# A hybrid block with a state space layer: the skip term, one normalization and the gate's buffers move

## The chip, the cores and the metric

The kernel runs on one core of a Trainium2 chip. A core has TensorE (PE: matrix products, with PEld for its loads of the stationary operand), VectorE (DVE), ScalarE (ACT), GpSimd (POOL) and SyncE (SP, which here issues most DMAs). PSUM is the memory that TensorE writes, used here as eight banks of 128 x 512 f32: two each under the tags A, B, C and T. The metric is the device time of one execution in microseconds. Runs are summed up by their median; one further execution was recorded by the profiler.

## The reference

Input x has 2 sequences of 2048 tokens with 256 features. Four residual layers follow each other, each on a normalized x: a state space layer, a mixture of 8 experts of which each token takes 2, an attention over a pair of tokens (over the two sequences), and the same mixture of experts again. Only the first layer is changed:

```python
zxbcdt = einsum('bld,ed->ble', layernorm(x), W_in)      # z: 512, xBC: 768, dt: 8
xBC = silu(causal_depthwise_conv(xBC, conv_w, conv_b))  # four taps
x, B, C = xBC[:512] as 8 heads of 64, xBC[512:640], xBC[640:]
dt = softplus(dt + dt_bias)
h_t = h_{t-1} * exp(dt * A) + (dt * x_t) B_t            # per head, state of 64 x 128
y = h_t C_t
y = y + D * x                                           # the skip: one number D per head
y = y * silu(z)                                         # the gate
y = y * rsqrt(mean(y * y) + eps) * norm_w
out = y @ W_out.T
```

## The kernel before

All of it is f32. Tokens are worked on in groups of 512 (TG), of four chunks of 128. There are eight groups, in the order (sequence 0, part 0), (sequence 1, part 0), (sequence 0, part 1) and so on (`order`), so 32 chunks, here counted from 0.

`project` makes a group ready. It normalizes x (`layernorm`: statistics and `xn` on VectorE, the power for `rs` on GpSimd), transposes `xn` on TensorE (`pt`, copied to `xT` by ScalarE), computes `dt` with a polynomial on VectorE, and then for six blocks of 128 channels the projection (`pc`, L1000), two copies of it on ScalarE (L1007, L1009), three taps of the convolution on VectorE (L1018) and a silu on ScalarE (L1026). The result is `xc`, with channels on the partitions.

`chunk_front` prepares one chunk: the gate `sz` = silu(`pz`) on ScalarE (L1050), the decay matrices `lt` of the eight heads (L1055, L1058, L1089), and `px`, the transpose of x to tokens on the partitions. VectorE reads `px` twice: `dtx` = dt * x (L1067) and `xd` = D * x (L1069). GpSimd makes `wx` from `dtx` (L1082).

`chunk_back` computes the chunk's output. `py` is C times the state (L1098), scaled into `y` by VectorE (L1100). The state `h` is scaled by GpSimd (L1109) and the product `ph` added by VectorE (L1111). `pi` is the product of `lt` and `dtx`, one matmul per head (L1114). Then GpSimd adds `xd` to `y` (L1121), VectorE adds `pi` (L1123), and GpSimd multiplies with `sz` (L1124). `chunk_out` squares `y` on ScalarE (L1133), transposes it (`pty`) and multiplies it with `W_out` (`po`), and VectorE adds the result to x (L1151).

The main loop interleaves by hand: per chunk it emits steps of the next group's `project` (`aside`), the front of the next chunk, the back of this one, and the output of the one before. Once a group is through the layer, `routing` chooses the experts of its tokens, and eight scatters per group (L438, GpSimd's queue) enter them in a table. These scatters are emitted by `late.step()`, one or none at each GpSimd step of a chunk. From about the fifth group on, expert tiles that are already full are computed between the chunks (`tiles.step()`; up products `pab` L727, down products `pf` L757, gate `gT` L736), 21 of them early.

SP's instructions stay in the program's order. Those of the other engines are put in order by a scheduler when the kernel is built; every engine then works through its own list in that order. Tiles come from pools with a number of buffers for each tag: `s2` has two unless `bufs` says otherwise. A tile's buffer comes free when all readers of its former content are done, so the number of buffers decides who waits.

Of the kernel before, what the change touches and what calls it, by code (L numbers as in the profile page):

```python
# [17 lines left out]
GT = 4  # L18
# [4 lines left out]
DI = 512  # L23
NH, HD = 8, 64
# [22 lines left out]
def kernel(  # L47
# [24 lines left out]
    nc = tc.nc  # L72
# [7 lines left out]
    lnp = ctx.enter_context(tc.tile_pool(name="ln", bufs=2))  # L80
# [6 lines left out]
    order = [(b, s) for s in range(NS) for b in range(NB)]  # L87
    xg, xr = {}, {}
# [22 lines left out]
    ident = const.tile([P, P], F32, name="ident")  # L111
# [47 lines left out]
    dsk = load_const("dsk", [P, NH], d_skip.partition_broadcast(P))  # L159
# [70 lines left out]
    def pool(i):  # L230
        on_pool[:] = [i.ins]


    normed, turned = [], []


    def layernorm(x, name):

        st = lnp.tile([P, GT, 6], F32, tag="st", name=f"st_{name}")
        mv = lnp.tile([P, GT, 2], F32, tag="mv", name=f"mv_{name}")  # L240
        for t in range(GT):
            nc.vector.bn_stats(st[:, t, :], x[:, t, :])
            nc.vector.bn_aggr(mv[:, t, :], st[:, t, :])
        yield
        rs = lnp.tile([P, GT], F32, tag="rs", name=f"rs_{name}")
        nc.vector.tensor_scalar(rs, mv[:, :, 1], EPS, None, ALU.add)  # L246
        pool(nc.gpsimd.tensor_tensor(rs, rs, mhalf, ALU.pow))  # L247
        yield
        xn = lnp.tile([P, GT, DM], F32, tag="xn", name=f"xn_{name}")
        for t in range(GT):  # L250
            i = nc.vector.tensor_scalar(
                xn[:, t, :], x[:, t, :], mv[:, t, 0:1], rs[:, t : t + 1], ALU.subtract, ALU.mult
            )
            normed[:] = [i.ins]
        return xn, rs, mv[:, :, 1]
# [606 lines left out]
    with tc.tile_pool(name="ssm1", bufs=1) as s1, tc.tile_pool(name="ssm2", bufs=2) as s2:  # L862
# [20 lines left out]
        def route_out():  # L883
# [23 lines left out]
                w_out_sb[:, :, DM:], pw[:, : DI // P * NE].rearrange("p (c n) -> p c n", n=NE)  # L907
            )

        sums = {g: tc.dram_tile([GT * NH, P], F32, name=f"sums{g[0]}{g[1]}") for g in order}  # L910
        tails, state = {}, {}
        for b in range(NB):
# [4 lines left out]

        def project(b, s):
            nm = f"{b}{s}"
            xn, rs, var = yield from layernorm(xg[b, s], f"a{nm}")  # L920
            yield
            xT = s2.tile([P, KD, TG], F32, tag="xT", name=f"xT_{nm}")
            transpose_group(xT, xn, f"a{nm}")
# [5 lines left out]
            for t in range(GT):  # L929
                for k in range(KD):  # L930
# [4 lines left out]
                        start=(k == 0),  # L935
                        stop=(k == KD - 1),
# [19 lines left out]
            r = s2.tile([P, GT, NH], F32, tag="r", name=f"r_{nm}")  # L956
# [5 lines left out]
            g = s2.tile([P, GT, NH], F32, tag="g", name=f"g_{nm}")  # L962
# [32 lines left out]
            xc = s2.tile([P, NC, TG], F32, tag="xc", name=f"xc_{nm}")  # L995
            nc.gpsimd.tensor_copy(pre[:, :, 0 : KC - 1], tails[b])
            for c in range(NC):
                pc = bank("A", f"pc_{nm}_{c}")
                for k in range(KD):
# [4 lines left out]
                        start=(k == 0),  # L1004
# [35 lines left out]
        def chunk_front(b, s, t, g, lb):  # L1040
            nm = f"{b}{s}{t}"
            xc, ts = g["xc"], slice(t * P, (t + 1) * P)
            per_head = [P, NH, HD]


            pz = bank("A", f"pz_{nm}")
            for k in range(KD):
                nc.tensor.matmul(pz, g["xT"][:, k, ts], w_in_sb[:, k, 0:DI], start=(k == 0), stop=(k == KD - 1))
            sz = s2.tile([P, DI], F32, tag="sz", name=f"sz_{nm}")
            nc.scalar.activation(sz, pz, AF.Silu)  # L1050


            lt = s2.tile([P, NH, P], F32, tag="lt", name=f"lt_{nm}", bufs=3)
            for i in range(NH):
                nc.scalar.activation(  # L1055
                    lt[:, i, :], lb[:, i, :], AF.Relu, bias=g["cum"][:, t, i : i + 1], scale=-1.0
                )
            nc.scalar.activation(lt, lt, AF.Exp, scale=-1.0)  # L1058


            px = bank("T", f"px_{nm}")
            for c in range(DI // P):
                nc.tensor.transpose(px[:, c * P : (c + 1) * P], xc[:, c, ts], ident)
            pxh = px.rearrange("p (h d) -> p h d", h=NH)
            dtx = s2.tile([P, DI], F32, tag="dtx", name=f"dtx_{nm}")
            dtxh = dtx.rearrange("p (h d) -> p h d", h=NH)
            nc.vector.tensor_tensor(dtxh, pxh, g["dt"][:, t, :].unsqueeze(2).to_broadcast(per_head), ALU.mult)  # L1067
            xd = s2.tile([P, DI], F32, tag="xd", name=f"xd_{nm}")
            nc.vector.tensor_tensor(  # L1069
                xd.rearrange("p (h d) -> p h d", h=NH), pxh, dsk.unsqueeze(2).to_broadcast(per_head), ALU.mult  # L1070
            )
            pb = bank("B", f"pb_{nm}")
            nc.tensor.transpose(pb[:, 0:P], xc[:, 4, ts], ident)
            nc.tensor.matmul(pb[:, P : 2 * P], xc[:, 4, ts], xc[:, 5, ts], start=True, stop=True)
            bt = s2.tile([P, P], F32, tag="bt", name=f"bt_{nm}")
            nc.scalar.copy(bt, pb[:, 0:P])
            gm = s2.tile([P, P], F32, tag="gm", name=f"gm_{nm}")
            nc.vector.tensor_tensor(gm, pb[:, P : 2 * P], tri, ALU.mult)


            wx = s2.tile([P, DI], F32, tag="wx", name=f"wx_{nm}")
            pool(nc.gpsimd.tensor_tensor(  # L1082
                wx.rearrange("p (h d) -> p h d", h=NH),
                dtxh,
                g["dec"][:, 2, t, :].unsqueeze(2).to_broadcast(per_head),
                ALU.mult,
            ))
            late.step()
            nc.vector.tensor_tensor(lt, lt, gm.unsqueeze(1).to_broadcast([P, NH, P]), ALU.mult)  # L1089
            return dict(lt=lt, dtx=dtx, xd=xd, bt=bt, wx=wx, sz=sz)  # L1090

        def chunk_back(b, s, t, g, f):
            nm = f"{b}{s}{t}"
            ts = slice(t * P, (t + 1) * P)
            per_head = [P, NH, HD]
            h = state[b]
            py = bank("C", f"py_{nm}")
            nc.tensor.matmul(py, g["xc"][:, 5, ts], h, start=True, stop=True)  # L1098
            y = s2.tile([P, DI], F32, tag="y", name=f"y_{nm}", bufs=3)
            nc.vector.tensor_tensor(  # L1100
                y.rearrange("p (h d) -> p h d", h=NH),
                py.rearrange("p (h d) -> p h d", h=NH),
                g["dec"][:, 0, t, :].unsqueeze(2).to_broadcast(per_head),
                ALU.mult,
            )
            ph = bank("C", f"ph_{nm}")
            nc.tensor.matmul(ph, f["bt"], f["wx"], start=True, stop=True)
            hh = h.rearrange("p (h d) -> p h d", h=NH)
            pool(nc.gpsimd.tensor_tensor(hh, hh, g["dec"][:, 1, t, :].unsqueeze(2).to_broadcast(per_head), ALU.mult))  # L1109
            late.step()  # L1110
            nc.vector.tensor_tensor(h, h, ph, ALU.add)  # L1111
            pi = bank("C", f"pi_{nm}")
            for i in range(NH):
                nc.tensor.matmul(  # L1114
                    pi[:, i * HD : (i + 1) * HD],
                    f["lt"][:, i, :],
                    f["dtx"][:, i * HD : (i + 1) * HD],
                    start=True,
                    stop=True,
                )  # L1120
            pool(nc.gpsimd.tensor_tensor(y, y, f["xd"], ALU.add))  # L1121
            late.step()
            nc.vector.tensor_tensor(y, y, pi, ALU.add)  # L1123
            pool(nc.gpsimd.tensor_tensor(y, y, f["sz"], ALU.mult))  # L1124
            late.step()
            return y

        def chunk_out(b, s, t, y):
            nm = f"{b}{s}{t}"

            yt = s2.tile([P, DI], F32, tag="yt", name=f"yt_{nm}")
            ss = s2.tile([P, 1], F32, tag="ss", name=f"ss_{nm}")
            nc.scalar.activation(yt, y, AF.Square, accum_out=ss)  # L1133
            nc.vector.tensor_scalar(ss, ss, 1.0 / DI, EPS, ALU.mult, ALU.add)
            pool(nc.gpsimd.tensor_tensor(ss, ss, mhalf[:, 0:1], ALU.pow))
            late.step()
# [3 lines left out]
            nc.scalar.copy(yt, pt)  # L1140
            po = bank("T", f"po_{nm}")
            for c in range(DI // P):
                nc.tensor.matmul(
                    po[:, 0 : DM + NE],
                    yt[:, c * P : (c + 1) * P],
                    w_out_sb[:, c, :],
                    start=(c == 0),
                    stop=(c == DI // P - 1),
                )
            x = xr[b, s][:, t, :]  # L1150
            nc.vector.scalar_tensor_tensor(x, po[:, 0 : DM + NE], ss, x, ALU.mult, ALU.add)  # L1151

# [402 lines left out]
```

## Time and profile before

| | us |
|---|---|
| median of 3 runs | 1716.64 (1710.98 to 1721.71) |
| the profiled execution's own time | 1689.27 |
| its span, first to last instruction | 1687.6 |
| PE busy over the span | 1579.0 |
| DVE busy | 896.0 |
| ACT busy | 672.3 |
| POOL busy | 740.2 |
| DMA queues: moved | 231.30 MB |

The profile's page gives busy times by engine, then the span in 40 slices of 42 us with the busy share in tenths, and then groups of like instructions. A line of such a group has the line of the program, the engine, the operation, what it writes and reads, how often, its busy time in us and the mean ns of one, and then the idle time of the engine just before it with what ended that. A matmul of f32 operands shows as two records, each with its load. The first layer ends at about 700 us, with the early expert tiles in its second half; the first expert layer ends before 900 us, the attention runs to about 1400 us beside the second layer's early tiles, and the second expert layer fills the rest.

### The profile page before, as it was taken

What the parts mean: (1) busy time and instruction counts of PE and PEld (TensorE: products, weight loads), DVE (VectorE), ACT (ScalarE), POOL (GpSimd) and SP (SyncE); (2) the same over time, 40 slices, a digit from 0 to 9 for tenths busy, and PEclk for the clock granted to TensorE, in tenths of its full rate; (3) what the DMA queues carried; (4) which work ended last, traced back from release to release, by engine and by line L of the source; (5) the groups of instructions that cost most, each with busy time, mean ns of one, the idle gap of its engine ahead of it and who ended that gap; (6) DMA issues with size and microseconds to landing.
All of it is one profiled execution on the core that took longest, in us unless ns stands there. A gap on an engine that the chain in (4) does not pass through costs nothing.

```text
span 1687.6 us, 22145 instructions
## 1 busy us (share of the span) xinstructions
PE 1579.0 (94%) x7088; PEld 1189.4 (70%) x7088; DVE 896.0 (53%) x2471; ACT 672.3 (40%) x1338; POOL 740.2 (44%) x702
## 2 busy tenths in 40 slices
PE   6997987999999999999998999899999999999997
PEld 4665555676677777788984566475767878888886
DVE  6777978847648364422227658548454622222222
ACT  5786867856647543232322202002020322323332
POOL 4356457455455566644442002423150663544443
PEclk9898988999999999999999999999999999999999
DMA  4022212743535455889852321715435588878883
GB/s 170 28 59 53 89 28 61 216 126 90 141 66 177 105 144 132 214 248 327 228 123 82 67 60 52 100 51 102 144 71 142 148 222 238 227 225 231 227 220 47
DMA packets 174744, 231.30 MB, mean 137 GB/s; under 512 B 45920, under 2 KB 138080, under 8 KB 174368
## 3 DMA queue, kind: packets, MB, share of 16 engines
q1 hardware_dynamic: 143520, 193.42, 38.8%
q0 software_dynamic: 31104, 36.42, 12.3%
q8 instruction: 58, 0.95, 0.2%
q14 instruction: 62, 0.51, 0.1%
HBM read 192.72 MB, written 37.06 MB: 136 GB/s over the span
## 4 chain that ended last, share of the span: by engine, by line
PE 46%; DMA 7%; DVE 2%; POOL 1%; issue 1%; ACT 0%; SPq 0%; DVEq 0%; POOLq 0%
PE pab_g L727 9%; PE pao L1446 7%; PE pq L1352 5%; PE pab_f L727 5%; PE pf_g L757 4%; PE pab_ge L727 3%; PE pvd L1426 3%; PE pk L1352 3%; DMA out_dram<-y_g,tab_g 2%; PE pf_f L757 2%; DMA o<-prob 2%; PE pf_ge L757 1%; PE pr_g L335 1%; DMA xs_f<-xnd_f,tab_f 1%; DMA resid<-y_f,tab_f 1%
## 5 line engine op out<-in xcount | busy, mean ns | idle before, releaser
L727 PE MATMUL pab_g<-xT_g,w_g 128*128 128x256 f32 (+1 forms) x896 | 181.4, 361 | 0.0
L727 PE MATMUL pab_fe<-xT_fe,w_fe 128*128 128x256 f32 x672 | 159.0, 392 | 20.0 <-DVE gT_fe L736 16.8
L727 PEld LDWEIGHTS pab_g<-xT_g,w_g 128*128 128x128 f32 x896 | 158.4, 190 | 19.6 <-ACT xT_g L718 0.4
L727 PEld LDWEIGHTS pab_fe<-xT_fe,w_fe 128*128 128x128 f32 x672 | 129.1, 195 | 47.3 <-DVE gT_fe L736 21.5
L781 POOL DMA_INDIRECT out_dram<-y_g,tab_g x51 | 80.3, 1575 | 137.2 <-DVE y_g L770 46.3
L735 ACT ACTIVATE sa_g<-pab_g,b_g 128x256 f32<-128x256 f32 (+1 forms) x112 | 51.0, 455 | 188.0 <-PE pab_g L727 188.0
L736 DVE SCALAR_TENSOR_TENSOR gT_g<-pab_g,b_g,sa_g 128x256 f32<-128x256 f32 (+1 forms) x112 | 51.5, 460 | 129.0 <-ACT sa_g L735 127.3
L1352 PE MATMUL pq<-w_qkv_sb,axT 128*128 128x512 f32 x256 | 117.4, 597 | 0.0
L1018 DVE SCALAR_TENSOR_TENSOR xc<-pre,conv_w_sb,xc 128x512 f32<-128x512 f32 x144 | 111.5, 791 | 4.2 <-ACT xc L1009 3.5
L1446 PE MATMUL pao<-w_o_sb,o 128*128 128x256 f32 x512 | 112.3, 380 | 0.0
L1446 PEld LDWEIGHTS pao<-w_o_sb,o 128*128 128x128 f32 x512 | 97.0, 190 | 15.9 <-issue 2.6
L727 PE MATMUL pab_f<-xT_f,w_f 128*128 128x256 f32 (+1 forms) x512 | 96.4, 346 | 0.0
L1000 PE MATMUL pc<-xT,w_in_sb 128*128 128x512 f32 x192 | 94.7, 622 | 0.2 <-ACT xc L1009 0.2
L438 POOL DMA_INDIRECT table_g<-pay_g,at_g x64 | 62.3, 974 | 72.5 <-DVE w_g L414 39.5
L757 PE MATMUL pf_g<-w_g,gT_g 128*128 128x256 f32 x408 | 92.8, 379 | 0.0
L727 PEld LDWEIGHTS pab_f<-xT_f,w_f 128*128 128x128 f32 x512 | 85.4, 191 | 9.4
L1055 ACT ACTIVATE lt<-lb,cum 128x128 f32<-128x128 f32 x256 | 82.9, 393 | 18.7 <-DMA lb<-sums 18.6
L1352 PEld LDWEIGHTS pq<-w_qkv_sb,axT 128*128 128x128 f32 x256 | 48.5, 192 | 57.9 <-issue 56.0
L781 POOL DMA_INDIRECT resid<-y_fe,tab_fe x42 | 67.0, 1596 | 37.0 <-DVE y_fe L770 21.8
L1367 ACT ACTIVATE kd<-pk 128x512 f32<-128x512 f32 x32 | 19.1, 597 | 159.5 <-PE pk L1352 90.5
L757 PEld LDWEIGHTS pf_g<-w_g,gT_g 128*128 128x128 f32 x408 | 75.4, 190 | 9.3 <-DVE gT_g L736 0.2
L247 POOL TENSOR_TENSOR rs_g<-rs_g,mhalf 128x4 f32<-128x4 f32 x8 | 8.2, 1019 | 167.6 <-DVE rs_g L246 151.9
(477 smaller groups left out, 3401.2 us busy)
## 6 DMA issues: line engine op xcount, KB each, us to landing
w_g<-in_wl_dram SPq DMA_DIRECT2D x28, 1024.0 KB, 6.0
w_fe<-in_wl_dram SPq DMA_DIRECT2D x21, 1024.0 KB, 5.0
lb<-sums SPq DMA_DIRECT2D x32, 512.0 KB, 5.3
w_f<-in_wl_dram SPq DMA_DIRECT2D x16, 1024.0 KB, 5.8
o<-prob SPq DMA_DIRECT2D x32, 512.0 KB, 17.9
w_g<-in_wl_dram SPq DMA_DIRECT2D x28, 512.0 KB, 4.9
w_fe<-in_wl_dram SPq DMA_DIRECT2D x21, 512.0 KB
w_ge<-in_wl_dram SPq DMA_DIRECT2D x9, 1024.0 KB
```

The lines of the kernel that those rows point to most:

```text
L438: i = nc.gpsimd.indirect_dma_start(out=self.table, out_offset=bass.IndirectOffsetOnAxis(ap=at[:, t, c : c + 1], axis=0), in_=pay[:, t, c, ...
L727: nc.tensor.matmul(p[:, q * n : (q + 1) * n], t["w1"][:, k, c * P : (c + 1) * P], t["xT"][:, k, :], start=(k == 0), stop=(k == KD - 1),)
L735: nc.scalar.activation(sa[:, :n], p[:, 0:n], AF.Silu, bias=t["b1"][:, i : i + 1])
L736: nc.vector.scalar_tensor_tensor(t["gT"][:, i, :n], p[:, n : 2 * n], t["b1"][:, NHT + i : NHT + i + 1], sa[:, :n], ALU.add, ALU.mult)
L757: nc.tensor.matmul(pos[h][:, h * DM : (h + 1) * DM], t["gT"][:, j, h * P : (h + 1) * P], t["w2"][:, j, :], start=(j == 0), stop=(j == NHT ...
L781: j = nc.gpsimd.indirect_dma_start(out=self.acc if self.direct else self.acc[: self.seq[i][4] or NT + TT, :], out_offset=bass.IndirectOffs ...
L1000: nc.tensor.matmul(pc, w_in_sb[:, k, DI + c * P : DI + (c + 1) * P], xT[:, k, :], start=(k == 0), stop=(k == KD - 1),)
L1018: nc.vector.scalar_tensor_tensor(xc[:, c, :], pre[:, c, j : j + TG], conv_w_sb[:, c, j : j + 1], xc[:, c, :], ALU.mult, ALU.add,)
L1055: nc.scalar.activation(lt[:, i, :], lb[:, i, :], AF.Relu, bias=g["cum"][:, t, i : i + 1], scale=-1.0)
L1352: nc.tensor.matmul(p, src[:, k, t * P : (t + 1) * P], w_qkv_sb[:, k, j, half * TG : (half + 1) * TG], start=(k == 0), stop=(k == KD - 1),)
L1426: nc.tensor.matmul(pvd, w_qkv_sb[:, k, 2, c * P : (c + 1) * P], xd[:, k, :], start=(k == 0), stop=(k == KD - 1),)
L1446: nc.tensor.matmul(po[:, j * DM : (j + 1) * DM], o[i][:, c, (t + j) * P : (t + j + 1) * P], w_o_sb[:, c, :], start=(c == 0), stop=(c == NA ...
```

## The change

It has three parts.

First, for the first five groups of `order` (`SKIPS = 5`, so chunks 0 to 19) the skip is computed on TensorE. Once at the start VectorE fills `skip`, four diagonal matrices of 128 x 128 with D on the diagonal (eight instructions on 64 partitions each). In `chunk_back` a matmul of `xc` with such a matrix is put ahead of each pair of `pi`'s heads; it writes the 128 columns that the two heads then add to. For these chunks `xd` and GpSimd's addition of it are gone, and with them one `late.step()` per chunk. For the last three groups they stay, but `xd` has one buffer instead of two.

Second, the normalization in `project` computes `xn` on ScalarE as x * rs + off, with `off` = -mean * rs from one small VectorE instruction. The other normalizations stay on VectorE.

Third, `sz` has three buffers instead of two.

```diff
+        if act:
+            off = lnp.tile([P, GT], F32, tag="off", name=f"off_{name}")
+            i = nc.vector.scalar_tensor_tensor(off, mv[:, :, 0], -1.0, rs, ALU.mult, ALU.mult)
+            normed[:] = [i.ins]
         for t in range(GT):
+            if act:
+                nc.scalar.activation(
+                    xn[:, t, :], x[:, t, :], AF.Identity, bias=off[:, t : t + 1], scale=rs[:, t : t + 1]
+                )
+                continue
             i = nc.vector.tensor_scalar(
                 xn[:, t, :], x[:, t, :], mv[:, t, 0:1], rs[:, t : t + 1], ALU.subtract, ALU.mult
             )
...
+        skip = s1.tile([P, DI // P, P], F32, name="skip")
+        for i in range(NH):
+            r = slice(i % 2 * HD, (i % 2 + 1) * HD)
+            nc.vector.tensor_scalar(skip[r, i // 2, :], ident[r, :], dsk[r, i : i + 1], None, ALU.mult)
...
-            xn, rs, var = yield from layernorm(xg[b, s], f"a{nm}")
+            xn, rs, var = yield from layernorm(xg[b, s], f"a{nm}", act=True)
...
-            sz = s2.tile([P, DI], F32, tag="sz", name=f"sz_{nm}")
+            sz = s2.tile([P, DI], F32, tag="sz", name=f"sz_{nm}", bufs=3)
...
-            xd = s2.tile([P, DI], F32, tag="xd", name=f"xd_{nm}")
-            nc.vector.tensor_tensor(
-                xd.rearrange("p (h d) -> p h d", h=NH), pxh, dsk.unsqueeze(2).to_broadcast(per_head), ALU.mult
-            )
+            xd = None
+            if order.index((b, s)) >= SKIPS:
+                xd = s2.tile([P, DI], F32, tag="xd", name=f"xd_{nm}", bufs=1)
+                nc.vector.tensor_tensor(
+                    xd.rearrange("p (h d) -> p h d", h=NH), pxh, dsk.unsqueeze(2).to_broadcast(per_head), ALU.mult
+                )
...
             for i in range(NH):
+                c = i // 2
+                if f["xd"] is None and i % 2 == 0:
+                    nc.tensor.matmul(
+                        pi[:, c * P : (c + 1) * P], g["xc"][:, c, ts], skip[:, c, :], start=(i == 0), stop=False
+                    )
                 nc.tensor.matmul(
                     pi[:, i * HD : (i + 1) * HD],
                     f["lt"][:, i, :],
                     f["dtx"][:, i * HD : (i + 1) * HD],
-                    start=True,
-                    stop=True,
-                )
-            pool(nc.gpsimd.tensor_tensor(y, y, f["xd"], ALU.add))
-            late.step()
+                    start=f["xd"] is not None,
+                    stop=f["xd"] is not None or i == NH - 1,
+                )
+            if f["xd"] is not None:
+                pool(nc.gpsimd.tensor_tensor(y, y, f["xd"], ALU.add))
+                late.step()
             nc.vector.tensor_tensor(y, y, pi, ALU.add)
...
+        SKIPS = 5
```

More of the change, by code (lines that the diff above doesn't have):

```diff
@@ L234, with layernorm @@
     normed, turned = [], []
-    def layernorm(x, name):
+    def layernorm(x, name, act=False):
         st = lnp.tile([P, GT, 6], F32, tag="st", name=f"st_{name}")
```

## The prediction

> **What bounds the kernel now.** I read the page's slices first, then the table by stretches, then the waits and groups of the stage that changes. Between 0 and about 700 us lies the state space stage; everything after it is untouched.
>
> ```profile
> PE   6997987999999999999998999899999999999997
> DVE  6777978847648364422227658548454622222222
> PEclk9898988999999999999999999999999999999999
> ```
>
> A slice is 42 us. In the first seven, VectorE is as full as TensorE and the granted clock dips; from the eighth TensorE alone is at nine tenths. The chain that ended last is no help: followed back it stops at 705.8 us and has no piece before that. So I cut at the end of the addition y<-y,pi (L1123) of chunks 5, 9, 13, 17 (117.2, 181.8, 243.1, 306.7 us) and of chunks 19, 23, 27, 31. The columns are busy us (and instructions) of PE, PEld, DVE, ACT, POOL, then the clock, the DMA share and GB/s.
>
> ```profile
> 117.20:181.80 64.60, 53.73 (x236) 35.68 (x234) 53.34 (x134) 46.45 (x94) 34.24 (x32) 0.92 0.24 58
> 181.80:243.10 61.30, 53.34 (x237) 34.04 (x236) 49.09 (x130) 45.76 (x90) 33.33 (x32) 0.92 0.19 61
> 243.10:306.70 63.60, 53.29 (x234) 34.44 (x232) 55.60 (x155) 47.91 (x93) 38.99 (x36) 0.92 0.30 88
> 364.00:466.30 102.30, 94.98 (x443) 71.44 (x442) 64.16 (x168) 62.20 (x121) 53.98 (x48) 0.98 0.43 120
> 466.30:567.40 101.10, 94.60 (x444) 71.61 (x443) 61.70 (x163) 62.05 (x121) 52.97 (x46) 0.98 0.45 121
> ```
>
> A group of four chunks takes 63.2 us early: PE 53.5 busy, DVE 52.7, ACT 46.7, POOL 35.5. None is full; the pace passes between them. Late, with one early expert tile in each chunk, a group takes 101 us and PE is busy 93%: there TensorE is the bound. Where the pace goes early, the groups and waits of 60 to 300 us show:
>
> ```profile
> L438 POOL DMA_INDIRECT table_f<-pay_f,at_f x24 | 28.8, 1201 | 4.2 <-issue 4.1 <-DVE st_f L242 0.2
> L1121 POOL TENSOR_TENSOR y<-y,xd 128x512 f32<-128x512 f32 x16 | 22.3, 1395 | 5.6 <-DVE y L1100 4.9 <-ACT yt L1140 0.4
> L1123 DVE TENSOR_TENSOR y<-y,pi 128x512 f32<-128x512 f32 x16 | 10.8, 676 | 11.8 <-POOL y L1121 7.2 <-PE pi L1114 4.6
> L1069 DVE TENSOR_TENSOR xd<-px,dsk 128x512 f32<-128x512 f32 x16 | 10.9, 679 | 0.0
> L251 DVE TENSOR_SCALAR xn_a<-x,mv_a,rs_a 128x256 f32<-128x256 f32 x12 | 9.4, 827 | 0.0
> L1114 PEld LDWEIGHTS pi<-dtx,lt 128*128 128x128 f32 x256 | 33.8, 208 | 7.9 <-DVE y L1100 4.9 <-issue 2.5 <-DVE h L1111 0.2
> L1050 ACT ACTIVATE sz<-pz 128x512 f32<-128x512 f32 x16 | 9.5, 593 | 18.7 <-POOL y L1124 18.6
> ```
>
> VectorE runs without a gap through the convolution and routing of a group. Then eight routing scatters (L438) come onto POOL between the y and h steps, and POOL sets the pace: the timeline has it working almost without a gap over 142.4 to 158.4, 205.3 to 224 and 263.9 to 271.9 us, 43 of 189.5 us. In these stretches stand four additions y<-y,xd (149.2, 205.3, 216.2, 270.7), and VectorE's y<-y,pi waits for two of them, 7.2 us.
>
> **The change, per early group.**
>
> VectorE loses four xd, 4 x 0.679 = 2.7 us. It loses four xn_a: 9.4 us for 12, so 3.1 us. It gains one small off (128x4; its likeness L941 takes 0.15 to 0.39), 0.2. Sum -5.6 of 52.7. Here a rule bears: the Trainium skill, "SBUF — State Buffer", section "SBUF: two separate sides", says that a VectorE instruction using two ports and a GpSimd instruction lock each other out for a whole instruction. The trace agrees in size: xn_a has a median of 408 ns over the stage but a longest of 2470, and a mean of 827 in this stretch. By the undisturbed median the move returns 1.6 us a group, by the row with its lock-outs 3.1; I take 3.1, because the disturbed time is what the group pays. Worth something is only what lies outside the POOL-paced stretches, 146.5 of 189.5 us: 5.6 x 0.77 = 4.3.
>
> POOL loses four y<-y,xd, 4 x 1.395 = 5.6 of 35.5. On the path were four in three groups, 4 x 1.27 / 3 = 1.7. y<-y,pi then waits for PE pi alone (already last of the two for 4.6 us). POOL also steps the routing scatters one time fewer per chunk (four instead of five). In the built order they stand almost as before, 16 of them instead of 15 or 18 around chunk 15, and the first early plan falls after 15 state additions instead of 16: nothing for it. SP's queue keeps its order.
>
> ScalarE gains four 128x256 instructions with a scale and a bias per partition. Bounds: by_fe (L769, 128x256, one such operand) 0.510, xc (L1009, 128x512, two) 0.784; I take 0.55, near the first, so 2.2 us. Against this speaks the Trainium skill, "ScalarE: Activation LUTs", section "Rules for kernel authors": additions and multiplications belong on VectorE, not ScalarE. By VectorE's 0.408 the move would lose 0.6 us a group if ScalarE set the pace; by the rows ScalarE idles 16.5 of 63.2 us, and its 2.2 lie in that. They wait for rs, which POOL makes, and for off; queued behind them on ScalarE are the Square of an earlier chunk, the next lt rows and the two xT copies, for which PE waits. The like wait of xn_f on POOL was 4.8 us in three times. If the idle time were used up, this costs 2.2 + 1.6 = 3.8 a group. The third sz buffer takes away the 18.6 us that ScalarE waited in five times; ScalarE was not the last there, so it only pays for the above: nothing by itself (0 to -1).
>
> TensorE gains four f32 matmuls of 128x128x128 per chunk, that is eight records. Bounds: pi's loads in a row cost 33.8 / 256 = 0.132 each, 1.06 a chunk; the 128-column pb matmuls (L1074) 6.3 / 32 = 0.197 each, 1.6 a chunk. They stand among pi's, so I take 1.06: 4.2 a group.
>
> Now the sum. VectorE and POOL would let a group shrink by 4.3 + 1.7 = 6.0, to 57.2. TensorE would then be asked for 53.5 + 4.2 = 57.7, more than there is. The best stretch of 60 us in the stage (60 to 120) had PE busy 57.1, 95%, at clock 1.00. So TensorE is late next: at the granted 0.92 its floor is 57.7 / 0.95 = 60.7 (-2.5); at a full clock 57.7 x 0.92 / 0.95 = 55.9 (-7.3). Fewer pauses should raise the clock: from 300 to 420 us, where the first tiles fill PE's pauses, it is 1.00. I take the midpoint, -4.9. The period of four groups (54 to 307 us) gives -19.6.
>
> Start: eight small VectorE instructions for skip (0.15 to 0.44 each, by L885 and L127), about 2 us, in a spot where VectorE waited 2.2 us for x: nothing, or +2. First norm on ScalarE: +0.5, within the error.
>
> Late: chunks 18 and 19 have the four matmuls where PE is full: 2 x 1.06 = +2.1. In groups 5 to 7 xd has one buffer. xd of chunk i+1 now waits for POOL's y<-y,xd of chunk i, which waits for y<-py on VectorE itself. In the built order xd therefore stands behind that y in six of twelve chunks; queued behind it are the h addition, y<-y,pi and gT of the expert tile, for which PE waits. The wait is what POOL needs after py (h 1.15, y<-y,xd 1.27) less VectorE's own 0.68 and 0.48: 1.3 us, and once or twice an indirect DMA of 1.2 more: 10 us of VectorE idle in all. VectorE is 60 to 63% busy there and mostly waits for PE's pi anyway; bounds 0 and +10, taken +2.5. px keeps its PSUM bank longer, but the next user of that bank, po of chunk i-1, comes some 12 us later.
>
> Sum: -19.6 + 2.1 + 2.5 = -15.0 on the profiled execution (1689.3, span 1687.6). The median of the runs is 1.6% above it, 1716.6, so -15.2 there: about 1701.5.
>
> **Rivals.** (a) The clock recovers fully and VectorE with POOL sets the pace: -6.0 x 4 + 2.1 = -22, 1694. For it: the 1.00 of 300 to 420 us; against: 0.92 in all three early groups. (b) TensorE takes the place of what is removed and the clock stays: -2.5 x 4 + 2.1 + 4 = -4, 1713. This is the change not doing what it says: work moved from two engines onto a third that was as full. For it: 53.5 against 52.7 busy. (c) Slower: the single xd buffer. Price: for each of twelve chunks POOL's h, one indirect DMA and y<-y,xd, 1.15 + 1.2 + 1.4 = 3.7, or 45, standing before gT, with PE stopped as it was for 14.2 us before pab_fe for want of gT (360 to 660 us). With the early gain that is -19.6 + 2.1 + 45 = +27, 1744. It decides once a wait outlasts the matmuls that PE has queued ahead of gT (some 3.5 us of pab). Against it: six of the twelve have no wait by the order.
>
> **How the numbers follow.** 38% for the forecast (own range 1692 to 1710), 22% for (a), 20% for (b), 20% for (c), spread over 1722 to 1755. Within 1% (17 us) is about what a measurement tells from no change: the runs of before lie 11 us apart. Faster: most of (a) and four tenths of the forecast, 0.35. Slower: most of (c), 0.17. Same: 0.48. For 8 in 10 the range goes from 1687 (half of (a)'s error below it) to 1738 (half of (c) above).
>
> **What would show it.** In the early groups: a period near 58 us; xd, y<-y,xd and the wait of y<-y,pi on POOL gone; sz without its wait; PE at 95% with a clock above 0.92; the xn rows on ACT near 0.55. Late: a group still at 101 us, VectorE's wait of xd on POOL of about 10 us in all, pab_fe's wait for gT no longer than 14 us. The prediction is wrong if the early period stays at 61 or more, or a late group passes 103.

## The result, and the profile after

| | before | after |
|---|---|---|
| median of 22 runs each | 1717.37 us (1705.72 to 1723.31) | 1721.90 us (1713.76 to 1731.11) |
| ratio to before, 95% interval | | 1.0033 (1.0018 to 1.0048) |
| profiled execution, its span | 1689.27, 1687.6 | 1713.76, 1712.1 |
| VectorE busy over the span | 896.0 | 867.4 |
| POOL busy | 740.2 | 709.2 |
| PE busy | 1579.0 | 1599.3 |

The change takes 29 us off VectorE and 31 us off POOL, and the kernel is 0.3% slower. The medians lie 4.5 us apart; by the ratio the loss is 5.7 us, where a gain of 15.2 was forecast. A warning belongs beside the table: the profiled execution of before, on which the prediction was built, lies 28 us below the median of its own kernel, under the fastest of the 22 runs, so the difference of the two profiles (24.5 us) overstates the loss. A second profile of before, taken later, spans 1703.6 us; it is used below where stages are compared.

The slices of after, a slice being 43 us, show where to look:

```profile
PE   7999998999899888899998999899999899999997
DVE  6777787457466364422226757447454622222222
PEclk9999999999999899999999999999999999999999
```

In the early slices the clock has lost its dips and PE stands at nine tenths. But slices 14 to 17, some 556 to 728 us, are now at eight tenths, where before had a row of nines, and in one of them the clock dips. The table by stretches, cut as in the prediction at the end of y<-y,pi (now L1146) of chunks 5, 9, 13, 17, then 19, 23, 27, 31, and at the first ordinary expert tile; columns as before: length, PE, PEld, DVE, ACT, POOL, clock, DMA share, GB/s.

```profile
119.10:176.10 57.00, 53.76 (x268) 35.96 (x267) 44.26 (x122) 45.65 (x93) 28.59 (x28) 1.00 0.20 68
176.10:231.70 55.60, 52.35 (x267) 35.66 (x266) 43.57 (x125) 45.42 (x93) 27.40 (x28) 1.00 0.24 63
231.70:291.20 59.50, 54.42 (x268) 37.18 (x267) 48.57 (x147) 45.66 (x93) 27.51 (x28) 0.97 0.19 56
...
351.70:446.50 94.80, 91.05 (x428) 68.41 (x427) 57.71 (x163) 64.83 (x123) 52.41 (x46) 0.98 0.44 119
446.50:553.20 106.70, 97.50 (x444) 73.52 (x444) 61.53 (x164) 64.55 (x123) 53.59 (x47) 0.95 0.41 115
553.20:654.60 101.40, 89.02 (x397) 70.30 (x396) 49.93 (x126) 34.96 (x73) 58.29 (x51) 0.92 0.45 114
654.60:751.60 97.00, 82.70 (x368) 68.47 (x367) 35.22 (x139) 25.49 (x52) 49.83 (x43) 0.93 0.68 177
```

The same view of before, for the last two of these stretches (chunks 28 to 31, and from there to the first ordinary tile):

```profile
568.10:653.10 85.00, 78.92 (x375) 62.97 (x374) 44.80 (x123) 34.99 (x71) 55.27 (x48) 0.96 0.46 117
653.10:735.50 82.40, 76.21 (x359) 63.76 (x358) 34.17 (x138) 24.89 (x50) 47.88 (x41) 1.00 0.80 210
```

The early half did what was forecast: 57.0, 55.6 and 59.5 us a group instead of 63.2, PE 91 to 94% busy, clock 0.97 to 1.00. From chunk 5 to 17 that is 172 us instead of 189.5. The second half gives it back. One group takes 106.7 us, but the one ahead of it took 94.8, and the two together are no longer than before (201.5 us against 203.4): work has moved between the windows. The loss stands behind them. The last group takes 101.4 us instead of 85.0, and from its start to the first ordinary tile it is 198.4 instead of 167.4, with 765 PE records instead of 734, more pauses and a lower clock. So the question is what the change did to a stage in which it changes almost no arithmetic.

### The profile page after: what moved, and what is told of

Read it like the earlier page. It is cut to its first block, busy times and chain, and to the rows that moved or that the text cites. A ratio compares the mean times of both kernels' runs of the same rounds, so it can differ in the third digit from the quotient of the medians.

```text
span 1712.1 us, 22393 instructions
## 1 busy us (share of the span) xinstructions
PE 1599.3 (93%) x7248; PEld 1206.8 (70%) x7248; DVE 867.4 (51%) x2435; ACT 679.7 (40%) x1366; POOL 709.2 (41%) x682
## 4 chain that ended last, share of the span: by engine, by line
PE 66%; DVE 11%; POOL 8%; issue 7%; DMA 5%; ACT 1%; SPq 1%; POOLq 0%; DVEq 0%; ACTq 0%
PE pab_g L736 9%; PE pao L1472 6%; PE pq L1378 6%; PE pab_f L736 5%; PE pab_fe L736 5%; PE pf_g L766 4%; PE pab_ge L736 3%; PE pk L1378 3%; DVE xc L1033 3%; PE pvd L1452 3%; PE pf_fe L766 3%; PE pf_f L766 2%; PE pc L1015 2%; PE pf_ge L766 2%; DMA out_dram<-y_g,tab_g 2%
## 5 line engine op out<-in xcount | busy, mean ns | idle before, releaser
L736 PE MATMUL pab_fe<-xT_fe,w_fe 128*128 128x256 f32 x672 | 166.2, 404 | 27.3 <-DVE gT_fe L745 14.4
L736 PEld LDWEIGHTS pab_fe<-xT_fe,w_fe 128*128 128x128 f32 x672 | 133.1, 203 | 58.9 <-DVE gT_fe L745 17.3
L1033 DVE SCALAR_TENSOR_TENSOR xc<-pre,conv_w_sb,xc 128x512 f32<-128x512 f32 x144 | 108.0, 762 | 12.5 <-ACT xc L1024 11.7
L1472 PE MATMUL pao<-w_o_sb,o 128*128 128x256 f32 x512 | 112.6, 380 | 0.2 <-issue 0.2
L790 POOL DMA_INDIRECT resid<-y_fe,tab_fe x42 | 71.9, 1712 | 60.1 <-DVE y_fe L779 51.2
L766 PE MATMUL pf_fe<-w_fe,gT_fe 128*128 128x256 f32 x336 | 79.7, 385 | 3.8 <-DVE gT_fe L745 3.6
```

What stands on the lines that cost most here:

```text
L736: nc.tensor.matmul(p[:, q * n : (q + 1) * n], t["w1"][:, k, c * P : (c + 1) * P], t["xT"][:, k, :], start=(k == 0), stop=(k == KD - 1),)
L766: nc.tensor.matmul(pos[h][:, h * DM : (h + 1) * DM], t["gT"][:, j, h * P : (h + 1) * P], t["w2"][:, j, :], start=(j == 0), stop=(j == NHT ...
L790: j = nc.gpsimd.indirect_dma_start(out=self.acc if self.direct else self.acc[: self.seq[i][4] or NT + TT, :], out_offset=bass.IndirectOffs ...
L1033: nc.vector.scalar_tensor_tensor(xc[:, c, :], pre[:, c, j : j + TG], conv_w_sb[:, c, j : j + 1], xc[:, c, :], ALU.mult, ALU.add,)
L1472: nc.tensor.matmul(po[:, j * DM : (j + 1) * DM], o[i][:, c, (t + j) * P : (t + j + 1) * P], w_o_sb[:, c, :], start=(c == 0), stop=(c == NA ...
```

## What the removed lines also did

The change takes out a GpSimd addition and the `late.step()` behind it. That call does not compute anything. It hands one step to the routing work, and the routing work of the third group ends by calling `plan_early`, which starts the early expert tiles. With four calls a chunk instead of five, this happens later in the program. The early tiles then go forward by `tiles.step()`, of which each chunk has three places: one ahead of the next chunk's front, one behind that front, one behind `chunk_back`. A tile has three steps, so it keeps the place at which the first one began. The numbers in the tile names count in the order of emission, and from them the program order of chunk 16 and of an ordinary chunk reads:

```
before  chunk 16: py y | PLAN | pi | [behind back] w | pe pc | pty po | ...
        later:    py y pi | [behind back] pf | pty po | [ahead of front] pxs gT pab0 pab1
                  | front: lb px | [behind front] pab2 pab3
after   chunk 16: py y pi | [behind back] nothing yet | pe pc | PLAN | pty po | ...
        later:    py y pi | [behind back] pab2 pab3 | pty po | [ahead of front] pf
                  | front: lb px | [behind front] pxs gT pab0 pab1
```

The plan crosses one place, and all tiles behind it move on by one place. The scheduler, which starts from this order, builds another list for TensorE. Chunk 27, where the difference is plain, from the built lists:

```
before  pi x8, pf x8, pty x4, pxs x4, pz, po x4, pab x8, pz, px x4, pb x2, pab x8, py, ph
after   pi x3, pxs x4, pi x5, pty x2, pab x16, pty x2, pf x3, pz x2, py, ph, po x4, pf x5, px x4, pb x2
```

Before, a tile's down product `pf` stands whole, behind the eight `pi`. After, sixteen `pab` follow each other, and the first three of `pf` come behind them with only two transposes between, split from the other five. Such a run of sixteen stands in three chunks of after's list (23, 27 and 28), and in before's only in the last one; `pf` is split for nine of the fifteen early tiles that begin between the chunks, and for one before. Whether this costs the time, or one of the parts of the change does, was put to the chip. In the experiments below, "before's place" and "after's place" name these two orders. From chunk 23 to the last `pi`, TensorE's built list is the same, matmul for matmul, in all five kernels with after's place. It is likewise the same in all kernels with before's place but one: with all parts and the calls kept, `pf` is split three times, and no sixteen `pab` stand in a row ahead of the last chunk.

## The experiments

Each batch was run on one chip beside the kernel before, whose median differed from batch to batch (1720, 1708, 1715 us), so only ratios are compared across batches. The stages are read from one profile each. "Late" in the expectations is chunk 17 to 31. That cut moves when the scheduler puts chunk 17's addition elsewhere, so the table has two cuts that hold nearly the same work: chunks 5 to 13 (two early groups), and chunk 13 to the first ordinary tile. The exception is the normalization alone, whose first cut has 422 PE records where before's has 471. The profiles of the first four experiments are long throughout: the rest behind that tile, which is the same in all of them, takes 971 to 976 us in them, and 960 in after and in the second profile of before.

| run | place | ratio (95%) | chunks 5 to 13 | 13 to first tile |
|---|---|---|---|---|
| before, second profile | before's | 1.0000 (0.9981 to 1.0019) | 125.7 | 499.1 |
| after | after's | 1.0033 (1.0018 to 1.0048) | 112.6 | 519.9 |
| two xd buffers | after's | 1.0025 (1.0012 to 1.0038) | 112.5 | 517.6 |
| skip alone | after's | 1.0024 (1.0013 to 1.0036) | 116.5 | 514.0 |
| normalization alone | before's | 1.0086 (1.0060 to 1.0111) | 121.8 | 513.0 |
| gate alone | before's | 1.0013 (0.9995 to 1.0030) | 121.5 | 510.5 |
| all parts, steps kept | before's | 0.9941 (0.9920 to 0.9962) | 115.5 | 494.0 |
| skip in 16 chunks | before's | 0.9919 (0.9890 to 0.9949) | 115.6 | 496.0 |
| skip in 17 chunks | after's | 0.9998 (0.9977 to 1.0020) | 115.4 | 506.3 |
| plan 2 steps later | before's | 1.0028 (1.0011 to 1.0044) | 126.8 | 505.6 |
| plan 3 steps later | after's | 1.0125 (1.0087 to 1.0162) | 125.8 | 530.4 |
| plan 4 steps later | third | 0.9987 (0.9966 to 1.0009) | 129.0 | 500.8 |
| skip alone, steps kept | before's | 0.9942 (0.9926 to 0.9958) | 119.0 | 502.1 |

### One part at a time

**Two buffers for xd** in the changed kernel (a small tile named row gave up one of its own for the room):

```diff
-                xd = s2.tile([P, DI], F32, tag="xd", name=f"xd_{nm}", bufs=1)
+                xd = s2.tile([P, DI], F32, tag="xd", name=f"xd_{nm}")
```

> The changed kernel with two buffers for xd again in the last three groups (and one instead of two for a small row, to have the room). Stretches between ends of y<-y,pi: early is chunk 5 to 17 (before 189.5, changed 172.2), late is chunk 17 to 31 (before 345.7, changed 363.3). If the single xd buffer is what gives the early gain back, xd's wait on POOL (14.4 us late) is gone, late falls to 345 to 352, and the kernel is 0.3 to 0.6% faster than before. If it is the order that was built for the late stage, or the normalization on ScalarE there, late stays at 358 or more and the time stays within 0.2% of the changed kernel's (1.003 of before).

Measured 1.0025: no different from the change as a whole, and the stage from chunk 17 to 31 at 359.5 us instead of 363.3. The single buffer, the prediction's own rival (c), is not the cause.

**The skip alone:** normalization on VectorE, two gate buffers, two xd buffers.

```diff
-            xn, rs, var = yield from layernorm(xg[b, s], f"a{nm}", act=True)
+            xn, rs, var = yield from layernorm(xg[b, s], f"a{nm}")
...
-            sz = s2.tile([P, DI], F32, tag="sz", name=f"sz_{nm}", bufs=3)
+            sz = s2.tile([P, DI], F32, tag="sz", name=f"sz_{nm}")
```

> The skip on TensorE for five groups alone: xd and sz with two buffers, the normalization on VectorE. By the sum of the prediction this part gives -2.7 x 0.77 - 1.7 per early group against TensorE's +4.2: early near 177 (between 172 and 185). Late: with two xd buffers and VectorE's normalization, near 348 if the single buffer or ScalarE's normalization is the cause of the loss; 358 or more if the order built around it is.

Measured 1.0024, with the whole early gain (173.2 us from chunk 5 to 17) and the whole late loss (359.9 from 17 to 31). Both come with the skip.

**The normalization alone,** and **the third gate buffer alone,** each put into the kernel before:

```diff
-            xn, rs, var = yield from layernorm(xg[b, s], f"a{nm}")
+            xn, rs, var = yield from layernorm(xg[b, s], f"a{nm}", act=True)
```

> The normalization on ScalarE alone, in all eight groups. Early by the prediction's sum: VectorE -2.9 x 0.77 = -2.2 per group, so 189.5 - 6.7 = 183. Late: if ScalarE's normalization is what loses there (it waits in ScalarE's order ahead of lt and the tiles' silu), late is 355 or more and the kernel slower than before; otherwise late is within 5 us of 345.7 and the kernel 0.2 to 0.5% faster.

```diff
-            sz = s2.tile([P, DI], F32, tag="sz", name=f"sz_{nm}")
+            sz = s2.tile([P, DI], F32, tag="sz", name=f"sz_{nm}", bufs=3)
```

> The third buffer of sz alone. The prediction gave it nothing: early 187 to 190, although ScalarE's 18.6 us of waiting on sz are gone. If the stall of ScalarE behind sz did set the pace (lt comes late after it), early falls by 5 us or more. Late within 5 us of 345.7 unless a new built order moves it.

The gate buffer alone changes nothing that can be measured (1.0013). The normalization alone is slower, 1.0086. From chunk 17 to 31 they take 341.5 and 340.8 us, so neither has the late loss by this cut. From chunk 5 to 17 they take 199.5 and 197.0 us, where 183 and 187 to 190 were expected; that cut ends later in their lists too, and the first two groups take 121.8 and 121.5. By the table's last column they stand at 513.0 and 510.5, above the 499.1 of before, which is from another batch whose rest is 1.2% shorter; these two profiles alone would not have decided it, and the runs below do. Why the normalization alone is slower stays open: its profiled execution, 1725.9 us, was 10 us faster than its median and within 3 us of the gate's, so the trace does not contain the loss. In the change as a whole it doesn't show, by the last run below; what it would do beside other changes was not tested.

### The calls kept, with everything else of the change

```diff
             if f["xd"] is not None:
                 pool(nc.gpsimd.tensor_tensor(y, y, f["xd"], ALU.add))
-                late.step()
+            late.step()
```

> The changed kernel with one line moved out of its condition: late.step() is called once per chunk there for the skip chunks too, as in the kernel before, though GpSimd's addition of xd is gone. Everything that is computed is as in the changed kernel. In the built order TensorE's list of the late stage (chunks 18 to 31) is then the one of before: the eight down products pf of a tile stand whole behind pi, and no sixteen pab in a row stand between them; the changed kernel's list splits pf ten times and has pab in runs of 16 there. Theory 'order' (the late stage lost its 14 to 18 us because the calls that went with the addition changed the built order): early stage (chunks 5 to 17) near 173 us, late stage (17 to 31) 342 to 350 instead of 363, the time 0.988 to 0.995 of before. Theory 'load' (the late stage is slower because TensorE arrives there hotter, with more matmuls and less clock, whatever the order): late stage stays at 358 to 363 and the time at 1.001 to 1.005.

Measured 0.9941 (0.9920 to 0.9962), 174.8 us early, 347.1 us from chunk 17 to 31. The same arithmetic as in the changed kernel, with one line outdented, is 0.9% faster than it. The stretch from chunk 17 to the first ordinary tile, of after and of this run:

```profile
291.20:751.60 460.40, 413.61 (x1878) 321.18 (x1877) 239.95 (x701) 231.50 (x453) 241.22 (x208) 0.94 0.52 140
```

```profile
292.90:727.60 434.70, 400.39 (x1879) 310.88 (x1878) 245.73 (x702) 225.80 (x447) 235.24 (x205) 0.98 0.53 139
```

The counts of PE records are equal, 1878 and 1879. After's 26 us more are 12.5 of pauses (46.8 against 34.3) and 13.2 of PE busy time at a clock of 0.94 instead of 0.98: 400.4 x 0.98 / 0.94 would be 417. These are single profiles; the two ratios put the difference at 0.9%, 16 us.

### One chunk across the edge

The skip alone for chunks 0 to 15, and for chunks 0 to 16:

```diff
-            if order.index((b, s)) >= SKIPS:
+            if order.index((b, s)) * GT + t >= 17:
```

(for 16 chunks the condition stays, with SKIPS = 4)

> The skip on TensorE alone (two xd buffers, two gate buffers, normalization on VectorE), for the first four groups, chunks 0 to 15, instead of five. The built late order is the one of before. Theory 'order': early stage 174 to 179 us (one chunk of twelve is as before), late stage 341 to 346, time 0.988 to 0.994 of before. Theory 'load': early stage the same, late stage near 358, time 1.000 to 1.004.

> As the run with chunks 0 to 15, but for chunks 0 to 16: one chunk more. The built late order flips with this one chunk to that of the changed kernel (pf split ten times, pab in runs of sixteen). Theory 'order': early stage 173 to 177 us, late stage 357 to 362, time 1.000 to 1.004 of before, so about 0.9% above the run with 16 chunks. Theory 'load': one chunk of skip is worth 1.1 us of TensorE; the two runs agree within 3 us in each stage.

> The kernel before, unchanged, for a second profile of it: the first one (1689 us) lay 28 us below the median of its own runs. Stages expected: early 189 to 199 us, late 340 to 347, from the last chunk to the first expert tile 82 to 98. If the late stage comes out at 355 or more here, the late loss of the changed kernel is only the difference between a fast execution and a usual one, and both theories fall. Time 1.000.

One chunk of skip more carries the plan across the place, and the ratio goes from 0.9919 to 0.9998, 0.8%. By stages the expectation for 16 chunks was missed: 170.4 us early instead of 174 to 179, and 356.8 late instead of 341 to 346. With 17 chunks all three figures fell just below theirs: 171.0 early, 356.5 late, ratio 0.9998. So the late stage by itself doesn't tell these two apart, and both are as theory 'load' had them (near 358, and within 3 us of each other); the ratio with 16 chunks, for which it had 1.000 to 1.004, decides against it. The difference stands in the stretch from chunk 31 to the first ordinary tile, 84.4 against 94.3 us. Part of what a late tile costs is paid there, since in after's place a tile's work is handed on past the last chunk (368 PE records there, 359 in before's). That is why the table's last column ends at the first ordinary tile; there the two are 496.0 and 506.3. The profile with 16 chunks lies besides at the upper end of its kernel's runs (1702.5 us against a median of 1696.3).

The second profile of before gave 189.3, 346.9 and 88.6 us for the three stages. So the late loss of after is real, and only the stretch behind chunk 31 of the first profile, 82.4 us, was unusually short.

### The place alone, with nothing of the change

The plan of the kernel before is emitted two, three or four late steps later; what is computed stays as it was.

```diff
             if n in EARLY:
+                for _ in range(3 if n == 3 else 0):
+                    yield
                 ffn.plan_early(n, EARLY[n], group[2])
```

> The kernel before, with nothing of the change, but the first early plan is emitted two late steps later (two yields ahead of plan_early for n = 3). In program order it still comes before the tiles.step() that stands behind chunk_back of chunk 16, so the steps of every early tile keep their places in the chunk: pab of parts 0 and 1 ahead of the next chunk's front, parts 2 and 3 behind it, pf behind chunk_back. Theory 'place' (what costs the late stage its time is the place in the chunk at which the early tiles' steps fall, and nothing else of the change): early stage 189 to 199 us, from chunk 17 to the first ordinary tile 430 to 441, time 0.997 to 1.003 of before. A theory by which any delay of the plan costs: above 1.005.

> As the run with two steps, with one step more: the plan now falls behind the tiles.step() that follows chunk_back of chunk 16, and every early tile's steps move on by one of the three places in a chunk, as in the changed kernel: pab 0 and 1 behind the front, pab 2 and 3 behind chunk_back, pf ahead of the next front. Nothing of the skip, the normalization or the gate is changed. Theory 'place': early stage as before (189 to 199 us), from chunk 17 to the first ordinary tile 450 to 460 us instead of 435, time 1.008 to 1.014 of before. If the place is not the cause: time 0.997 to 1.004, stretch 430 to 441.

> The third place: four steps later, pab 0 and 1 behind chunk_back, pab 2 and 3 ahead of the front, pf behind the front. In the built order the eight pf stand whole again behind ph or pi. Theory 'place', in the form that pf split and pressed between other work right behind its own pab is what costs: the stretch is near that of before, 432 to 445 us, time 0.997 to 1.006. If any place but that of before is bad: 450 us or more, and 1.008 or more.

Two steps leave the place and give 1.0028, just above no change; three steps cross it and give 1.0125; with four, the third place, it is 0.9987. So a delay as such is not what costs, the place is. Its price is 1.0125 / 1.0028, 1.0%. From chunk 22 to the last `pi`, TensorE's list with three steps is that of after, matmul for matmul. This is the stretch from chunk 17 to the first ordinary tile with two steps, and then with three:

```profile
309.40:751.00 441.60, 400.79 (x1866) 312.38 (x1865) 244.64 (x715) 226.95 (x447) 238.81 (x209) 0.97 0.52 142
```

```profile
307.60:774.10 466.50, 412.93 (x1867) 318.76 (x1866) 258.77 (x715) 231.56 (x451) 246.41 (x213) 0.95 0.51 138
```

The pattern of after again, in a kernel without any of it: 25 us more, half of it pauses (53.6 against 40.8), half of it busy time of the same records at a lower clock. The stretch came out longer than expected (450 to 460): the profile with three steps is the slowest of its six runs, 7.6 us above their median, and the two medians lie 18 us apart. What PE waits for there, in us, times and longest, with two steps and with three:

```profile
PE pab_fe L727 <- DVE gT_fe L736: 18.7, 14, 3.2
PE pab_fe L727 <- ACT xT_fe L718: 10.5, 5, 7.9
PE pxs_fe L714 <- DMA xs_fe<-xnd_f,tab_fe: 3.4, 3, 1.2
...
PE pk_f L368 <- DVE gT_fe L736: 1.6, 2, 0.9
PE pf_fe L757 <- DVE gT_fe L736: 1.2, 2, 0.9
```

```profile
PE pab_fe L727 <- DVE gT_fe L736: 15.6, 8, 4.4
PE pab_fe L727 <- issue: 8.7, 3, 7.3
PE pxs_fe L714 <- DMA xs_fe<-xnd_f,tab_fe: 6.2, 2, 5.0
PE pf_fe L757 <- DVE gT_fe L736: 3.8, 2, 3.1
PE pd L931 <- DVE gT_fe L736: 3.7, 1, 3.7
PE pk_f L368 <- DVE gT_fe L736: 3.1, 2, 2.8
PE pk_f L368 <- DVE sel_f L362: 2.9, 1, 2.9
PE pk_f L368 <- DVE sc_f L402: 2.7, 1, 2.7
```

No one line carries the loss. The wait of `pab` for `gT`, the stage's largest, is even smaller in all, but it comes in fewer and longer pieces. Waits that stood near nothing have grown: `pk`, a small product of the routing, waits 8.7 us in all instead of 1.6, `pd` 3.7, `pf` 3.8 instead of 1.2, the tile's transpose `pxs` 6.2 instead of 3.4 for its DMA. After shows the same (`pk` 6.0, `pf` 3.6, `pxs` 6.9; with the calls kept 2.1, 2.1 and 0.9).

What the place changes most is the length of single pauses: those of more than 2.5 us sum to 11.2 us with two steps and 40.0 us with three. One of the runs of sixteen `pab`, with three steps, halts in its middle, where the next `pab` waits for VectorE to take up the earlier ones:

```profile
470.59 3.62 PE L727 MATMUL pab_fe<-xT_fe,w_fe 128*128 128x256 f32 x16
478.56 5.41 PE L727 MATMUL pab_fe<-xT_fe,w_fe 128*128 128x256 f32 x16 [4.35 <-DVE gT_fe L736]
```

The view by stretches, cut at this pause, shows the clock at half speed behind it, though TensorE is fully busy again:

```profile
474.20:478.50 4.30, 0.01 (x1) 0.00 (x0) 0.63 (x2) 1.59 (x5) 3.92 (x5) 1.00 0.28 74
479.00:482.40 3.40, 3.40 (x10) 2.69 (x9) 0.16 (x1) 1.49 (x6) 0.89 (x1) 0.50 0.01 0
482.40:492.00 9.60, 9.60 (x38) 6.89 (x38) 3.45 (x7) 5.73 (x9) 3.48 (x4) 1.00 0.34 111
```

The three runs of sixteen have such a pause each (4.35, 4.35 and 3.77 us; in after 4.28, 4.29 and 3.75). In the whole stretch from chunk 17 to the first ordinary tile, the five kernels with after's place have 7 to 10 pauses of more than 2.5 us and 44 to 51 us at half speed. All other profiles have 1 to 4 and 14 to 31; the third place, with no run of sixteen and no split `pf`, has 3 and 20.5. With two and with three steps it is 23.9 and 51.2 us, and half of the difference, 13.7, is near the 12.1 us of busy time by which they differ. How much each change in the list contributes was not taken apart.

### The skip alone, with the calls kept

The edit is the outdented line shown above, in the kernel with the skip alone.

> The skip alone for chunks 0 to 19 (two xd buffers, two gate buffers, normalization on VectorE) with late.step() kept for these chunks, so that the early tiles' steps keep the places of before. Theory 'place': early stage 171 to 175 us, from chunk 17 to the first ordinary tile 434 to 441, time 0.990 to 0.994 of before; beside the run of all three parts with the steps kept (0.994) it says what the single xd buffer, the normalization on ScalarE and the third gate buffer add up to: nothing, or up to 0.3%.

Measured 0.9942, against 0.9941 with all three parts. Normalization on ScalarE, third gate buffer and single xd buffer together add up to nothing that these runs can measure. The early stage came out at 185.3 us, not 171 to 175. In part this is the cut: the third group's window has 284 PE records where after's has 268, because the addition that ends it stands later in the list; the two groups before it hold the work of after's, and take 119.0 us (after 112.6, second profile of before 125.7), so part of the miss is real. The stretch behind is as expected, 435.8.

### The sum

Four pairs compute the same, up to one chunk of skip, and differ in when late steps are taken, and so in the place: all parts, 1.0033 to 0.9941; the skip alone, 1.0024 to 0.9942; 17 and 16 chunks, 0.9998 to 0.9919; before itself, 1.0125 to 1.0028. The place costs 0.9, 0.8, 0.8 and 1.0%; the first two pairs join ratios of different batches, the last two stand in one batch each. With the place kept, the change gains 0.6%, 10 us. The place takes 0.9%, 16 us, if priced by the first pair, which gives the measured +0.3% by construction; by the other three pairs the sum is +0.2 to +0.4%. Three of the versions with before's place beat the kernels before and after; the skip in the first 16 chunks alone, with nothing else, has the lowest ratio, 0.9919, and its interval overlaps those of the two runs at 0.994.

## Why the prediction was wrong, point by point

**What held.** The early group was put at 58 us and came to 57.4 in the mean. TensorE's share of the sum held: it was busy 53.8 and 52.4 us at a full clock in the first two groups, with 268 and 267 records. Before had 53.7 and 53.3 for 236 and 237 records at 0.92, which is 49.4 and 49.1 at a full clock; the 30 records more thus cost 3.3 to 4.3 us, where 4.2 was taken. That the total came so near is in part luck. The clock, taken halfway between 0.92 and 1.00, went to 0.99; with it the working gives about 56, and TensorE's busy share, taken as 95%, was 93% and made up for it. VectorE came down by 7.2 us a group and GpSimd by 7.7, where 5.6 was taken for each. Rival (a), a full clock with VectorE and GpSimd setting the pace, had 57.2 for this group: the early half doesn't tell it from the forecast. The groups of after between 60 and 300 us:

```profile
L1146 DVE TENSOR_TENSOR y<-y,pi 128x512 f32<-128x512 f32 x17 | 11.6, 683 | 8.0 <-PE pi L1136 8.0
L1065 ACT ACTIVATE sz<-pz 128x512 f32<-128x512 f32 x17 | 10.1, 594 | 0.1
L256 ACT ACTIVATE xn_a<-x,off_a,rs_a 128x256 f32<-128x256 f32 x13 | 6.9, 586 | 3.3 <-DVE off_a L252 3.3
```

y<-y,pi no longer waits for POOL, sz no longer waits at all, and xn on ScalarE takes 0.586 us where 0.55 was taken. Its one wait for off took 3.3 us.

**The single xd buffer** was put at 10 us of VectorE's idle time and 2.5 us of the end, within 0 and +10. The waits of VectorE from chunk 17 to 31 in after have it:

```profile
DVE xd L1086 <- POOL y L1144: 14.4, 5, 4.4
```

That is 14.4 us in five waits, and with two buffers the time is the same within the intervals (1.0025 against 1.0033). So the waits came as described, and the 2.5 us are neither borne out nor refuted. Rival (c), slower by the single buffer, had the sign of the result, for a reason that is not the cause.

**The step that failed** is the sentence that priced the calls: "POOL also steps the routing scatters one time fewer per chunk (four instead of five). In the built order they stand almost as before, [...] and the first early plan falls after 15 state additions instead of 16: nothing for it." The missing call was seen and costed at nothing, and the count read for it can't show what it does. In the traces the plan's first VectorE instruction stands behind 15 state additions in after and also with the calls kept, at 250.7 and 252.5 us; before has 16, and so has the kernel with the plan three steps later. What matters is the program order, where the plan comes later, past one place of `tiles.step()`. The step was not followed to what the plan starts: the early tiles, of three steps each, all moved on by one place. This one term measured +16 us (0.8 to 1.0% by the four pairs), more than the gain that the change has without it. The late part of the sum, "where PE is full: 2 x 1.06 = +2.1", rested on the same assumption, that the late list of TensorE stays as it was. The built list of the changed kernel, with its sixteen `pab` in a row and its split `pf`, contradicts it without any run.

**The size of the rest.** With the place kept the gain was 10 us by the ratio, and 14 us by the profiles of the same batch (spans 1689.3 and 1703.6), against 15 forecast. One profile can't settle 4 us; the ratio's interval goes from -0.4 to -0.8%, 7 to 14 us, and 15 lies just outside. The sign that the prediction itself had named for being wrong, a late group above 103 us, came in (106.7), while the other, an early period of 61 or more, did not. They pointed to the right half, but the late sign was set by one fast profile: the second profile of before, unchanged, has a group of 104.7 us.

**The profile it was built on** did no harm to the early cuts (125.8 and 125.7 us for two groups in the two profiles of before). It does to a comparison of late stages: by the first profile after loses 32 us from chunk 17 to the first ordinary tile, by the second 25.

## What to carry to other kernels

Where work is interleaved by counters that other code advances, a removed instruction can take a tick of the counter with it; follow every such tick to what it starts, and compare the built lists in the stages that the change does not mean to touch. When work is moved off one engine and the gain is missing, cut the time into stages first: a gain of 17 us and a loss of 18 look like no effect until they are seen apart. And an order that came about by accident can be tested by itself, by delaying what starts it in the unchanged kernel.

## What the runs showed of the hardware that was not expected

A long pause of TensorE was paid for more than once in this kernel: the granted clock fell after it. With equal counts of matmul records, the stretch with 53.6 us of pauses also had 12 us more of busy time, at a granted clock of 0.95 instead of 0.97; after against the run with the calls kept shows the same (46.8 and 34.3 us of pauses, 13 us of busy time, 0.94 and 0.98). In these two pairs the time lost was about twice the added pauses. The other way round, the early groups went from a clock of 0.92 to 0.97 and 1.00 when PE's busy share rose from 83 to 87% to 91 to 94%.

The traces also show which comes first. Cut finely, the clock in the late stage is 1.00 or 0.50, and it stays at 0.50 for 3.4 to 6.8 us in after and with three steps. There 18 of the 19 falls come 1.9 to 5.3 us after the beginning of a pause of more than 2.5 us, and every such pause is followed by one. With two steps, three of five falls stand behind no pause so long, so this is not the only way to a fall; what brings those about stays open.
